# A macaron block on one core: v laid out by head pair and row half, light products with v in 64x64 parts, router in column groups

## The chip, the cores and the metric

The kernel runs on one core of a Trainium2 chip. The metric is the device time of one execution in microseconds. The kernel before took 1715.18 us, the median of 3 runs (1710.5 to 1721.73).

## What is computed

Eight sequences of 1024 rows of 256 numbers, all in 32 bits, go through a feed-forward layer with 8 experts, an attention layer and the same feed-forward layer again. Cut to what matters here:

```
x = x + 0.5 * ffn(layernorm(x))
x = x + attn(layernorm(x))
x = x + 0.5 * ffn(layernorm(x))

ffn:   logits = x @ router_w + router_b            # 256 -> 8
       the two best experts of each row, softmax over the two
       sum of gate * (gelu(x @ W1[e] + b1[e]) @ W2[e] + b2[e])
attn:  light: q, k, v = split(layernorm(x) @ wqkv_l)   # 8 heads of 64
              windows of 64 rows; each attends to itself and to the windows before and after
              softmax(q k^T / 8) @ v, then @ wo_l
       heavy: the 256 best rows for q and the 256 best for k, v, by two scores of each row
              full attention among them, 8 heads of 64, then @ wo_h, added to the rows of q
```

## The kernel before

Everything is written as recorded operations: `record` (line 189, so most profile lines carry L221), `copy` (L304, an eviction from PSUM on VectorE or ScalarE), `scale` (L313, VectorE or GpSimd) and `count`. `Plan` then orders all operations of the program with a list scheduler of its own (`schedule`, line 453; `backward`, 569; `order`, 617). It prices each operation (`Op.cost`, `Engine.work` at line 227 for TensorE, with a fixed charge for a change of the array's shape), looks ahead a number of operations on each engine, chooses VectorE or ScalarE for each eviction and gives PSUM banks of the pool `pmm` in the order in which they come free. What order it starts from is set at the end of `program` (lines 1993 on): each stage (rows, experts, front, heavy, project, light, last sum, dense) has a place and a length in units of one sequence, moved by the table `PLACES` (line 77). Any change of an operation or of a place can so move every instruction on every engine.

PSUM has eight banks of 128 x 512 numbers: `psim` two tiles of two banks (scores), `pmm` three single banks (everything else), `pexp` one (the experts' first product, `ph`). Pools are at lines 685 to 687.

A matmul of 32-bit numbers shows as two records in the profile, a transpose as one. A matmul may use a part of the array: the rows that its contraction needs and the columns that its stationary side needs. "128*64" in a profile line is 128 rows by 64 columns.

The parts that the change and the prediction touch:

- `logits` (line 1176, tiles `pl`): for a group of 4 tiles of 128 rows, 8 matmuls, each with 128 rows of x as the stationary side and the router's 8 columns as the moving side, into one bank; then one addition of the bias on VectorE. It is called from `rows` (line 941, for the 14 routed passes over a sequence) and from `dense` (line 1206, for the first pass of sequence 0 and the last pass of sequence 7, in which all experts are computed).
- `project` (line 1769, tiles `lv`, `lk`, `lq`): v of a tile of 128 rows is two matmuls of 128*128 with 512 moving columns; partition p of `v[:, t, :]` is row p of tile t, all heads side by side.
- `scores_light` (line 1401, tiles `sim_..atl`): for a tile t and a group g of four heads, 24 matmuls at most of 64*64 (row half j is the head of a pair, column half w is the window of queries), with 64, 128 or 192 moving keys. The keys of head j = 0 and j = 1 stand in different orders (`OWN`, `OTHER`, line 1396).
- `soften` (line 1323): one maximum over the four heads on VectorE, four exponentials with sums on ScalarE, a reciprocal, and `scale`.
- `values_light` (line 1438): four transposes of a head's own 128 keys (`keys_first`, tile `pa`), two of the keys beside (tile `pb`), both evicted (`at`, `bt`); then into one bank `pav` four matmuls of 128*64 over the own keys (two at a time, one in each column half) and up to eight of 64*64 over the keys beside, of which row half and column half are always the same, j. Where the window beside lies in the wrong row half of v, its copy `vside` is read, which two DMAs on SyncE's queue make for each tile (`prepare`, line 1827). One eviction makes `loT`, then `lo` multiplies with wo_l.
- `attend_heavy` (line 1360): scores of two head pairs in a `psim` tile, `soften`, eight transposes, the product with v, for 2 tiles of queries and 2 groups in each of 8 sequences: 32 times.

```
psim = nc.pool(ctx, "psim", 2, space=PSUM)
pmm = nc.banked(ctx, "pmm", 3, space=PSUM)
pexp = nc.pool(ctx, "pexp", 1, space=PSUM)
```

Of the kernel before, what the change touches and what calls it, by code (L numbers as in the profile page):

```python
# [44 lines left out]
F32 = mybir.dt.float32  # L45
# [12 lines left out]
P = 128  # L58
# [18 lines left out]
PLACES = {  # L77
    2: (-0.006, 0.000),
    8: (-0.109, 0.000),
    12: (0.000, 0.094),  # L80
    13: (0.143, 0.000),
    16: (0.442, 0.000),
    22: (0.000, -0.182),
    23: (-0.119, -0.119),
    24: (-0.004, 0.000),
    26: (0.000, 0.405),
    31: (0.000, -0.063),
    44: (0.038, 0.000),
    47: (0.000, 0.055),
    48: (0.051, 0.000),  # L90
    54: (0.044, 0.000),
    55: (0.000, -0.120),
    57: (0.040, 0.040),
    62: (0.014, 0.014),
    69: (0.086, 0.000),
    70: (0.403, 0.000),
# [85 lines left out]
class Engine:  # L182
# [44 lines left out]
    def work(method, out, ins, kw):  # L227
# [430 lines left out]
def program(  # L658
# [80 lines left out]
    rw_sb = load(router_w, "rw_sb")  # L739
# [201 lines left out]
    def rows(f, src, group, routed):  # L941
# [11 lines left out]
        rank = small([P, T, E], "erank")  # L953
        for i_b, b in enumerate(group):
# [7 lines left out]
            for hf in range(2):  # L962
# [13 lines left out]
                logits(ls[:, ts(hf, 4), :], yT, 4, f"{n}_{hf}")  # L976
# [184 lines left out]
    def better(ls, rank, tiles, n):  # L1161
# [12 lines left out]
        nc.vector.tensor_reduce(rank, gt, axis=AX.X, op=ALU.add)  # L1174

    def logits(dst, yT, tiles, n):
        pl = bank(f"pl_{n}")
        for i in range(tiles):
            for k in range(KD):
                nc.tensor.matmul(  # L1180
                    pl[:, ts(i, E)],
                    yT[:, k, ts(i, P)],
                    rw_sb[:, k, :],
                    start=(k == 0),
                    stop=(k == KD - 1),
                )
        nc.vector.tensor_tensor(
            dst,
            pl[:, : tiles * E].rearrange("p (t e) -> p t e", e=E),
# [16 lines left out]
    def dense(rows_of, weights, n, yT=None):  # L1206
# [26 lines left out]
        logits(lg, yT, m, n)  # L1233
        rank = sized(two, [P, m, E], F32, "cmp2", f"erank_{n}", NT * slots(MOST) // 2)
# [88 lines left out]
    def soften(sim, keys, n):  # L1323

        nmax = three.tile([P, 4], F32, tag="nmax", name=f"nmax_{n}")
        nc.vector.tensor_reduce(
            nmax.rearrange("p (c j) -> p c j", c=2),
            sim.rearrange("p j c k -> p c j k"),
            axis=AX.X,
            op=ALU.max,  # L1330
            negate=True,
        )
        pool, tag = (one, "ah") if keys > 3 * W else (two, "a")
        a = pool.tile([P, 4, keys], F32, tag=tag, name=f"a_{n}")
        asum = three.tile([P, 4], F32, tag="asum", name=f"asum_{n}")
        for c in range(2):
            for j in range(2):
                i = 2 * c + j
                nc.scalar.activation(
                    a[:, i, :],  # L1340
                    sim[:, j, c, :],
# [713 lines left out]
```

## Time and profile before

| What | Value |
|---|---|
| median of 3 runs | 1715.18 us |
| the profiled execution: its time, its span | 1724.71 us, 1723.0 us |
| granted TensorE clock, mean | 0.988 |
| TensorE busy | 1635.0 us (95%) |
| VectorE, ScalarE, GpSimd busy | 1232.4, 879.8, 836.7 us |
| bytes moved by DMA | 284.60 MB, 165 GB/s mean |
| TensorE busy from 0 to 150 us / 600 to 1100 us | 128.46 us / 483.38 us |

The profile is of one execution, on a clock that starts with its first instruction. "Busy" is the union of the records' times; records of TensorE overlap, so that their durations (about 0.27 us for a 128-column one) are longer than the distance from one start to the next, and it is this distance that counts for throughput. The chain of work that ended last is followed back from the last instruction; a line of it gives start, time until the next piece, and what ran.

### The profile page before, as it was taken

To read this page: it belongs to the slowest core of one execution; us is meant where nothing else is said; L and a number is where in the kernel's file an instruction comes from. 1 tells how busy PE (TensorE), PEld (TensorE's weight loads), DVE (VectorE), ACT (ScalarE), POOL (GpSimd) and SP (SyncE) were. 2 spreads that over 40 slices of the span, in tenths; PEclk is the share of its full clock that TensorE was granted. 3 is DMA by queue.
4 is the path that set the end of the run, shared out by engine and by line. 5 is a ranking of instruction groups with operands and counts; after the bars stand their busy time and mean duration, and the time that the engine had idled before them with its cause. 6 is when DMAs were issued, how large, how long until landed. Compare 5 with 4: busy or idle time off the path is not lost.

```text
span 1723.0 us, 39326 instructions
## 1 busy us (share of the span) xinstructions
PE 1635.0 (95%) x13849; PEld 1221.9 (71%) x13849; DVE 1232.4 (72%) x3881; ACT 879.8 (51%) x2500; POOL 836.7 (49%) x721
## 2 busy tenths in 40 slices
PE   7899999999999999999999999998999999999998
PEld 4566787656777677776777776677677776668786
DVE  6677748798876597658758797547876598568645
ACT  1123737534655565546656545466456554455532
POOL 1050576165553325558466625456373566453424
PEclk9899999999999999999999999999999999999999
DMA  9364786223662335787585623657366555644453
GB/s 190 134 199 152 217 268 196 86 77 118 199 211 74 80 113 158 238 244 228 157 248 173 171 90 108 207 174 230 126 190 198 139 158 181 212 126 129 128 169 113
DMA packets 220037, 284.60 MB, mean 165 GB/s; under 512 B 53448, under 2 KB 160864, under 8 KB 219584
## 3 DMA queue, kind: packets, MB, share of 16 engines
q1 hardware_dynamic: 190896, 208.77, 39.5%
q0 software_dynamic: 28368, 73.31, 15.4%
q8 instruction: 109, 1.79, 0.4%
q14 instruction: 88, 0.72, 0.1%
q10 hardware_dynamic: 576, 0.02, 0.0%
HBM read 196.15 MB, written 80.61 MB: 161 GB/s over the span
## 4 chain that ended last, share of the span: by engine, by line
PE 68%; DVE 15%; DMA 11%; issue 4%; POOL 1%; ACT 1%; SPq 0%; POOLq 0%; DVEq 0%; ACTq 0%
PE po_0f L221 3%; PE ph_0f L221 2%; PE po_7f L221 2%; PE po_2f L221 2%; PE ph_7f L221 2%; PE po_6f L221 2%; PE po_4f L221 2%; PE ph_6f L221 1%; PE ph_4f L221 1%; PE ph_2f L221 1%; DMA got_6at<-ys_6f,at_6f 1%; PE lk_3at L221 1%; DMA xp_6f<-y_6f,token_6f 1%; PE pt_6f L221 1%; PE lk_6at L221 1%
## 5 line engine op out<-in xcount | busy, mean ns | idle before, releaser
L221 POOL DMA_INDIRECT xp_2f<-y_2f,token_2f x78 | 82.2, 1053 | 97.1 <-DVE token_2f L221 40.5
L221 ACT ACT_TABLE_LOAD x75 | 96.2, 1283 | 3.8 <-DVE nmax_5atl L221 1.5
L221 POOL DMA_INDIRECT xp_6f<-y_6f,token_6f x62 | 67.5, 1088 | 53.1 <-PE pt_6f L221 26.0
L221 POOL DMA_INDIRECT xp_4f<-y_4f,token_4f x62 | 66.2, 1068 | 40.6 <-issue 16.3
L221 POOL DMA_INDIRECT xp_0f<-y_0f,token_0f x39 | 40.6, 1040 | 35.2 <-PE pt_0f L221 10.9
L221 PE MATMUL ph_2f<-xTe_2f,wt_2f 128*128 128x128 f32 x312 | 45.5, 279 | 2.6 <-DMA wt_2f<-wpk 2.6
L221 ACT ACTIVATE act_0f<-ph_0f,b_sb 128x512 f32<-128x512 f32 x16 | 11.0, 687 | 70.9 <-PE ph_0f L221 53.2
L221 PEld LDWEIGHTS ph_2f<-xTe_2f,wt_2f 128*128 128x128 f32 x312 | 41.2, 191 | 8.4 <-DMA wt_2f<-wpk 4.9
L221 DVE SCALAR_TENSOR_TENSOR x_last<-po_7f,weight_7f,x_last 128x256 f32<-128x256 f32 x64 | 27.9, 479 | 23.9 <-PE po_7f L221 23.7
L221 PE MATMUL po_2f<-wt_2f,act_2f 128*128 128x256 f32 x156 | 44.5, 381 | 0.3 <-ACT act_2f L221 0.3
L313 POOL TENSOR_TENSOR a_1atl<-a_1atl,asum_1atl 128x768 f32<-128x768 f32 x11 | 17.0, 1544 | 50.9 <-DVE asum_1atl L221 44.0
L221 PE MATMUL ph_0f<-qT,experts 128*128 128x512 f32 x64 | 36.4, 695 | 2.4 <-ACT act_0f L221 2.4
L221 PE MATMUL ph_7f<-yTf_7f,experts 128*128 128x256 f32 x128 | 34.6, 386 | 4.0 <-ACT act_7f L221 4.0
L221 PEld LDWEIGHTS ph_4f<-xTe_4f,wt_4f 128*128 128x128 f32 x248 | 34.1, 191 | 5.6 <-issue 3.7
L221 PE MATMUL ph_4f<-xTe_4f,wt_4f 128*128 128x128 f32 x248 | 37.8, 278 | 0.2 <-DMA wt_4f<-wpk 0.2
L221 PE MATMUL po_0f<-experts,act_0f 128*128 128x256 f32 x128 | 35.7, 384 | 0.9 <-ACT act_0f L221 0.9
L221 ACT ACTIVATE act_7f<-ph_7f,b_sb 128x256 f32<-128x256 f32 x32 | 15.2, 474 | 41.5 <-PE ph_7f L221 25.0
L221 PE MATMUL po_7f<-experts,act_7f 128*128 128x256 f32 x128 | 36.4, 378 | 0.0
L221 POOL DMA_INDIRECT xp_1f<-y_1f,token_1f x23 | 23.9, 1039 | 25.3 <-DVE ends_1f L221 12.7
L221 PE MATMUL ph_6f<-xTe_6f,wt_6f 128*128 128x128 f32 x248 | 35.6, 277 | 0.6 <-DMA wt_6f<-wpk 0.6
L221 PEld LDWEIGHTS ph_6f<-xTe_6f,wt_6f 128*128 128x128 f32 x248 | 32.9, 191 | 4.6 <-issue 2.1
L221 PE MATMUL po_6f<-wt_6f,act_6f 128*128 128x256 f32 x124 | 35.0, 380 | 0.3 <-ACT act_6f L221 0.3
(1493 smaller groups left out, 5800.0 us busy)
## 6 DMA issues: line engine op xcount, KB each, us to landing
wt_2f<-wpk SPq DMA_DIRECT2D x78, 256.5 KB
wt_4f<-wpk SPq DMA_DIRECT2D x62, 256.5 KB
wt_6f<-wpk SPq DMA_DIRECT2D x62, 256.5 KB
wt_0f<-wpk SPq DMA_DIRECT2D x39, 256.5 KB
ys_2f<-yp_2f SPq DMA_DIRECT2D x38, 256.0 KB
ys_4f<-yp_4f SPq DMA_DIRECT2D x30, 256.0 KB
ys_6f<-yp_6f SPq DMA_DIRECT2D x30, 256.0 KB
o<-h_b SPq DMA_DIRECT2D x56, 128.0 KB
```

The lines of the kernel that those rows point to most:

```text
L221: op = Op(self.plan, engines, lambda _: issue(*args, **kw), outs, ins, kind, **how)
L313: return getattr(nc, engine).tensor_tensor(dst, dst, by, op=ALU.mult)
```

## The change

1. v is laid out anew. `project` makes it with matmuls of 128*64: partition half c of `v[:, t, :]` holds, for window w at column 256 w, the 64 rows of the window for the heads of pair c of each group. All keys of a head pair so stand in one row half.
2. `soften` writes the light weights as [64-key block, head pair, pair member, key], so that one transpose gives the keys of pair c = 0 in the upper and those of c = 1 in the lower row half. `values_light` makes six transposes: four into `pa`, two into the columns of the score tile that the scores leave free (`room`, 128 columns of each bank); both are evicted. All products with v are then 64*64: row half c, column half j, four parts one after the other. The two row halves write two banks, `pav[0]` and `pav[1]`, and there are two evictions for `loT`. `pb`, `vside` and its DMAs are gone.
3. The heavy scores no longer lie in `psim` but in two `pmm` banks, one for each j, with a maximum for each.
4. `logits` swaps sides: the router's weights, padded with zeros to 32 columns, are stationary, 128 rows of x move, and tile i goes to column group i. The result is evicted, transposed back and added to the bias. `rank` is written in 16 bits.
5. The planner's price list gets an entry for 32 columns, and `PLACES` goes from 19 entries to 51.

```diff
 PLACES = {
+    0: (-0.035, -0.035),
     2: (-0.006, 0.000),
-    8: (-0.109, 0.000),
...
@@ work @@
+        if cols <= 32:
+            return {"work": n / 2.4, "array": (128, 32)}
         if array == (64, 64):
             return {"work": 58 * n / 64, "array": array}
@@ program @@
-    rw_sb = load(router_w, "rw_sb")
+    rw_sb = cons.tile([P, KD, 4 * E], F32, tag="rw_sb", name="rw_sb")
+    nc.vector.memset(rw_sb, 0.0)
+    nc.scalar.dma_start(out=rw_sb[:, :, :E], in_=router_w)
@@ better @@
-        nc.vector.tensor_reduce(rank, gt, axis=AX.X, op=ALU.add)
+        nc.count(rank, gt)
@@ logits @@
-    def logits(dst, yT, tiles, n):
+    def logits(dst, yT, spare, tiles, n):
         pl = bank(f"pl_{n}")
-        for i in range(tiles):
-            for k in range(KD):
+        for k in range(KD):
+            for i in range(tiles):
                 nc.tensor.matmul(
-                    pl[:, ts(i, E)],
-                    yT[:, k, ts(i, P)],
-                    rw_sb[:, k, :],
+                    pl[4 * E * i : 4 * E * (i + 1), :P],
+                    rw_sb[:, k, :],
+                    yT[:, k, ts(i, P)],
...
+        some = 4 * E * tiles
+        turned = spare[:some, :P]
+        evict(turned, pl[:some, :P])
+        nc.tensor.transpose(pl[:, P : P + some], turned, ident[:some, :some])
         nc.vector.tensor_tensor(
             dst,
-            pl[:, : tiles * E].rearrange("p (t e) -> p t e", e=E),
+            pl[:, P : P + some].rearrange("p (t e) -> p t e", e=4 * E)[:, :, :E],
@@ soften @@
-        a = pool.tile([P, 4, keys], F32, tag=tag, name=f"a_{n}")
+        parts = keys // W if light else 1
+        a = pool.tile([P, parts, 4, keys // parts], F32, tag=tag, name=f"a_{n}")
...
-                    a[:, i, :],
-                    sim[:, j, c, :],
+                    a[:, :, i, :],
+                    sim[j][:, c, :].rearrange("p (b k) -> p b k", b=parts),
@@ attend_heavy @@
-            sim = psim.tile([P, 2, HALF], F32, tag="sim", name=f"sim_{n}_{g}")
-            sim = sim.rearrange("p j (c k) -> p j c k", c=2)
+            sim = [bank(f"sim_{n}_{g}_{j}").rearrange("p (c k) -> p c k", c=2) for j in range(2)]
@@ scores_light @@
         sim = psim.tile([P, 2, HALF], F32, tag="sim", name=f"sim_{n}_{g}")
+        room = sim[:, :, 6 * W :]
...
-            apart = []
             for w in range(2):
                 for j in range(2):
-                    if w in beside and w != j:
-                        score(c, w, j, 0, q0 - W * j, 3 * W)
-                        continue
-                    score(c, w, j, OWN[j], q0, P)
-                    if w in beside:
-                        apart.append((c, w, j, OTHER[j], q0 - W if w == 0 else q0 + P, W))
-            for one_of in apart:
-                score(*one_of)
+                    score(c, w, j, 0, q0, 3 * W if w and w in beside else P)
+            if 0 in beside:
+                for j in range(2):
+                    score(c, 0, j, P, q0 - W, W)
@@ values_light @@
-        at = keys_first(a, OWN, f"{n}_{g}_0")
-        pb = bank(f"pb_{n}_{g}")
...
+        pa = bank(f"pa_{n}_{g}")
+        for i in range(6):
+            to = pa[:, ts(i, P)] if i < 4 else room[:, i - 4]
+            pair = a[:, i // 2, i % 2 * 2 : i % 2 * 2 + 2, :].rearrange("p c k -> p (c k)")
+            nc.tensor.transpose(to, pair, ident)
+        at = three.tile([P, 4, P], F32, tag="at", name=f"at_{n}_{g}")
+        evict(at.rearrange("p i q -> p (i q)"), pa)
+        bt = two.tile([P, 2, P], F32, tag="bt", name=f"bt_{n}_{g}")
+        evict(bt, room)
+        pav = [bank(f"pav_{n}_{g}_{c}")[:, :P] for c in range(2)]
...
+        for w in range(2):
+            for c in range(2):
+                for j in range(2):
+                    value(
+                        c, j, t, w, at[half(c), 2 * w + j, :], slice(0, P), start=(w == 0), stop=False
+                    )
+        for w in beside:
+            for c in range(2):
+                for j in range(2):
+                    value(
+                        c,
+                        j,
+                        t + 2 * w - 1,
+                        1 - w,
+                        bt[half(c), j, half(w)],
+                        half(w),
+                        start=False,
+                        stop=(w == beside[-1]),
+                    )
         for c in range(2):
...
-        evict(loT[:, ts(g, 2), :].rearrange("p c q -> p (c q)"), pav[:, : 2 * P])
+            evict(loT[:, 2 * g + c, :], pav[c])
@@ project @@
-            for k in range(KD):
-                nc.tensor.matmul(
-                    pv,
-                    xT[:, k, ts(t, P)],
-                    wqkv_sb[:, k, 2 * INNER :],
+            for w in range(2):
+                for k in range(KD):
+                    for c in range(2):
+                        of = wqkv_sb[:, k, 2 * INNER :].rearrange("p (g c i) -> p g c i", g=2, c=2)
+                        nc.tensor.matmul(
+                            pv[half(c), ts(w, 2 * P)],
+                            xT[:, k, t * P + w * W : t * P + (w + 1) * W],
+                            of[:, :, c, :],
...
@@ light, prepare @@
-            vside = two.tile([P, KI, DH], F32, tag="vside", name=f"vside_{n}_{t}")
-            for w, src in enumerate((t - 1, t + 1)):
-                if 0 <= src < NT:
-                    nc.sync.dma_start(
-                        out=vside[w * W : (w + 1) * W, :, :],
-                        in_=v[(1 - w) * W : (2 - w) * W, src, :].rearrange(
-                            "p (c j d) -> p c j d", c=KI, j=2
-                        )[:, :, w, :],
-                    )
```

More of the change, by code (lines that the diff above doesn't have):

```diff
@@ L1232, in dense @@
         lg = sized(two, [P, m, E], F32, "cmp2", f"lg_{n}", NT * slots(MOST) // 2)
-        logits(lg, yT, m, n)
-        rank = sized(two, [P, m, E], F32, "cmp2", f"erank_{n}", NT * slots(MOST) // 2)
+        logits(lg, yT, two.tile([P, D], F32, tag="y", name=f"turned_{n}"), m, n)
+        rank = sized(two, [P, m, E], BF16, "cmp2", f"erank_{n}", NT * slots(MOST))
         better(lg, rank, m, n)
```

166 lines of the change are left out of this document (90 added, 76 removed).

## The prediction

> **What bounds the kernel now.** I read the page first: busy times and the shares of the chain.
>
> ```profile
> span 1723.0 us, 39326 instructions
> PE 1635.0 (95%) x13849; PEld 1221.9 (71%) x13849; DVE 1232.4 (72%) x3881; ACT 879.8 (51%) x2500; POOL 836.7 (49%) x721
> ...
> PE 68%; DVE 15%; DMA 11%; issue 4%; POOL 1%; ACT 1%; SPq 0%; POOLq 0%; DVEq 0%; ACTq 0%
> ```
>
> TensorE (PE) is busy 95% of the span and carries 68% of the chain. Next, what TensorE waits for:
>
> ```profile
> PE pt_0f L221 <- DVE y_0f L221: 12.6, 3, 8.7
> PE pt_6f L221 <- DMA xp_6f<-y_6f,token_6f: 5.5, 3, 3.5
> PE ph_7f L221 <- ACT act_7f L221: 4.0, 6, 0.9
> PE ph_1f L221 <- DMA wt_1f<-wpk: 2.8, 1, 2.8
> ```
>
> The longest wait is at the start; then there are only many small ones. So TensorE's throughput is the price of everything. It is read from distances between starts, here from the chain of waits (start, time until the next piece, what):
>
> ```profile
> 328.32 2.10 PE pav_0atl L221 x48
> 1016.79 1.75 PE pl_3f L221 x16
> ```
>
> Sixteen router records take 1.75 us, 0.109 each, though each moves only 8 columns. Two light value steps take 2.10 us. What parts of the array give is in the timeline (start, length, what):
>
> ```profile
> 516.65 1.57 PE L221 MATMUL sim_1atl<-kT,qT 64*64 64x128 f32 x48
> ...
> 792.49 1.09 PE L221 MATMUL pav_2atl<-at_2atl,v 128*64 128x128 f32 x16
> 793.51 0.27 PE L221 MATMUL pav_2atl<-bt_2atl,vside_2at 64*64 64x64 f32 x1
> 793.52 0.27 PE L221 MATMUL pav_2atl<-bt_2atl,v 64*64 64x64 f32 x1
> 793.62 0.22 PE L221 MATMUL pav_2atl<-bt_2atl,vside_2at 64*64 64x64 f32 x1
> 793.63 0.22 PE L221 MATMUL pav_2atl<-bt_2atl,v 64*64 64x64 f32 x1
> 793.68 0.22 PE L221 MATMUL pav_2atl<-bt_2atl,vside_2at 64*64 64x64 f32 x1
> ```
>
> The 16 records over the own keys (128*64) go in pairs, 0.109 from pair to pair: 8 x 0.109 + the last one's length. Those over the keys beside also go in pairs (793.51 and 793.52, 793.62 and 793.63, then 0.059 apart), because only two of the four 64x64 parts are used. The 48 score records, 128 columns in the mean, take 1.57 us: twelve rounds of four at 0.109 plus one length of 0.27 is 1.58. There, four parts do work at once. Between 792.49's last pair (793.31) and 793.51 there are 0.20 instead of 0.109, and the first new pair loses another 0.05: a change of the array's shape costs 0.15 here, up to 0.25 elsewhere; I take 0.19.
>
> I price every matmul in the built order of the kernel before by such rows (128 columns 0.109 a record, 256 columns 0.216, 512 columns 0.429, pairs and fours as above, 425 changes of shape at 0.19). That gives 1582 us of the 1723; 141 are waits, some 20 of them half clock.
>
> **The change, part by part.**
>
> *Values over the keys beside.* 896 matmuls, 1792 records. Now 896 pairs x 0.059 = 52.9; in fours 448 x 0.059 = 26.4. Saved 26.4.
>
> *Values over the own keys.* 1024 records in 512 pairs x 0.109 = 55.8; after, a contraction of 64 needs twice the records, 2048, in 512 fours x 0.109 = 55.8. Nothing. Bounds for both products: four at once as in the score row (26.4 saved together), or only two at once as in the rows of the keys beside (own keys 1024 pairs, 111.6: 55.8 lost together). I take the score row: it has the same parts, two row halves in two banks, back to back.
>
> *Transposes.* 768 before and after. Nothing.
>
> *v.* 128 matmuls x 2 x 0.429 = 109.8 become 512 in pairs of two column halves, 512 pairs x 0.216 = 110.6. Costs 0.8.
>
> *Router.* 512 records x 0.109 = 55.8. After, 512 records in four column groups and 34 transposes x 0.109 = 3.7. No row has column groups of 32. Bounds: four at once, 128 x 0.109 = 14.0, and one at a time, 55.8; with two at a time, 27.9. So -38.1 to +3.7. I take four at once, since column halves overlap fully in the value row and quarters of the array in the score row.
>
> *Changes of shape.* The new built order has 414, among them 72 into or out of the column groups, which are more than paid by the own keys now having the shape of the scores. 11 x 0.19 = 2.1 saved.
>
> Work on TensorE: 26.4 + 38.1 + 2.1 - 0.8 = 65.8 less.
>
> *Evictions and VectorE.* ScalarE gets 109 more copies, VectorE 53 and 32 more maxima (of half the size). The row for a 128x256 copy is 0.37 us on ScalarE, 0.42 on VectorE: below 41 and 36 us, to 55% and 76% of the shorter span. They lie beside TensorE; without that cover, 77. The strided exponentials (row 0.43 each, 512 of them) may cost 0 to 0.1 more, 51 us on an engine that is half idle; 0. The 16-bit rank: 0.
>
> The Trainium skill ("TensorEngine Tiling (Array Packing)", Performance Considerations, PSUM Bottleneck) speaks against the change here: tiling speeds up TensorE but not the emptying of PSUM, which may become the limit. By the rows ScalarE is 51% busy and the copies are covered; if the rule held and the 162 copies stood on the path at 0.37, the sum below would be 60 worse, about 1735.
>
> *DMAs.* 112 issues of vside leave SyncE's queue (0.606 us each, 68 us of the queue; the wt loads and h_a stand behind them). TensorE's waits for DMAs that the view lists sum to about 17 us, a third of it wt. 0 to 5 saved; 2.
>
> *New holds of PSUM.* This is the loss. Heavy scores now keep two of the three pmm banks until their exponentials are done:
>
> ```profile
> 790.34 1.22 DVE L221 TENSOR_REDUCE nmax_3ath<-sim_3ath 128x4 f32<-128x1024 f32 x1
> ...
> 792.95 0.48 ACT L221 ACTIVATE a_3ath<-sim_3ath,nmax_3ath 128x256 f32<-128x256 f32 x1
> ```
>
> From 790.3 to 793.4: 3.1 us, with a signal to TensorE about 3.5. In the new order the TensorE work between the last heavy score in a bank and the next use of that bank is 3.0 us in the median, 1.9 in the lowest tenth; before, the psim tile had 6 us and more. The sum of what lacks to 3.5 is 42 us over 64 banks, 21 a pair. The heavy transposes stand 5.7 us of work behind the scores (median) instead of 13, and need about 6; this is late in the same places. For ordinary evictions (1.1 us needed; 0.8 for the halved pav ones) what lacks grows in pmm from 56 to 66 us, in psim from 0 to 3, where the room must be emptied before the next scores. The router's new transpose waits for its eviction, and the expert products queued behind it on TensorE wait too: 1.15 us of other work stand between in the median, and 6 us lack over 34 calls. Sum: 21 + 10 + 3 + 6 = 40. One wait often serves two tiles, so I take 28. Ends: 0, and 32 holds x 3.3 = 106 with nothing beside them.
>
> *Order and PLACES.* All stages move; what that does is in the counts above, which come from the new order. Start and end look alike: the same first products, dense experts at the end.
>
> Sum: -65.8 - 2 + 28 = -40. Profiled execution 1724.7 -> about 1685; it lay 9.5 above the median, so the median goes from 1715 to **1675**. Its own range, from waits of 10 to 48 (all 40 and a fifth more) and DMAs of 0 to 5: 1654 to 1697.
>
> **The rivals.**
>
> *A. Column groups do not overlap.* For it: no row of 32 columns. Against it: pairs of 64 columns do. Two at a time adds 14, one at a time 42: 1689 to 1717, at the mean 1703. "No change" is the far end, with the evictions added.
>
> *B. Heavy scores starve TensorE (the other side).* Place: 32 holds in the heavy stage, two of three banks gone, one left for everything. Price: up to 3.3 us a hold. It decides from 68 / 32 = 2.1 us a hold, where all that is saved is given back; at 3.3 the time is 1715 - 68 + 106 = 1753. Against it: psim and pexp go on (light scores, first expert products), and 3.0 us of work stand there in the order. For it: VectorE at 76% answers late.
>
> *C. Waits shrink too.* With SyncE's queue lighter and light scores no longer sharing psim with heavy ones, the 141 us of waits don't grow: 1715 - 68 - 5 = 1642.
>
> *D. Value parts run only two at a time.* 1675 + 26 + 56 = 1757. Against it: the score row. I give it 2 in 100, with B.
>
> **How the numbers follow.** Forecast 0.63 at 1675, A 0.13 at 1703, B and D 0.11 above 1715, C 0.13 at 1642. The range takes in forecast, A and C: 1640 to 1712, leaving out B and D, and the ends. Faster by over 1% (about what a measurement of this kernel can tell from no change; below 1698): 0.60 of the forecast, C, and 0.05 of A: 0.78. Within 1%: 0.03 + 0.07 and 0.01 of B: 0.11. Slower: 0.11.
>
> **What would show it.** Right: two value steps are 64 records in about 1.5 us (8 x 0.109 + 8 x 0.059 + 0.15) instead of 48 in 2.10; a router call's 16 records take 0.45 to 0.7 us plus a transpose; TensorE's busy time falls by 50 to 70 us; no vside in the DMA list. Waits of TensorE that name heavy exponentials, a_..ath or nmax_..ath, and evictions of loT sum to some 20 to 40 us. Wrong: pl records 0.109 apart (A); waits of 3 us in each heavy stage (B); value records in pairs (D).

## The result, and the profile after

The changed kernel takes 1775.38 us (median of 4 runs, 1769.31 to 1780.66), the kernel before 1716.98 (4 runs, 1710.5 to 1721.73): a ratio of 1.0342, with a 95% interval from 1.029 to 1.0393. The forecast was 1675, with a range up to 1712. The profiled execution of the changed kernel took 1769.31 us, with a span of 1767.6 and a granted clock of 0.983.

First the page of the changed kernel: span, busy times, and the shares of the chain.

```profile
span 1767.6 us, 42906 instructions
...
PE 1642.7 (93%) x15675; PEld 1239.2 (70%) x15675; DVE 1249.8 (71%) x3964; ACT 925.9 (52%) x2621; POOL 839.9 (48%) x724
...
PE 60%; DVE 15%; DMA 11%; issue 7%; POOL 3%; ACT 2%; SPq 1%; POOLq 0%; DVEq 0%; ACTq 0%
```

TensorE was to lose 50 to 70 us of busy time. It gained 8 (1635.0 to 1642.7), and it also stands idle for longer: by the gaps between its records 112.6 us instead of 74.8. What it waits for (waited for, total, times, longest):

```profile
PE pt_0f L254 <- DVE y_0f L254: 9.9, 2, 8.5
PE pt_2f L254 <- DMA xp_2f<-y_2f,token_2f: 7.8, 3, 3.1
PE pa_7ath L254 <- POOL a_7ath L348: 3.8, 1, 3.8
PE ph_7f L254 <- ACT act_7f L254: 3.7, 7, 0.6
PE pc_6f L254 <- DVE chosen_6f L254: 3.6, 1, 3.6
```

The longest one at the start is as before, one heavy wait in this list is new (pa_7ath), and no wait is large. The prediction named a sign: waits for heavy exponentials (a_..ath) or an eviction of loT would sum to 20 to 40 us. Those over 0.15 us sum to 15.2, against 3.3 before. So both parts of the loss have to be read from distances between starts. Here is the timeline of TensorE where a light step came as the forecast had it (start, length, what):

```profile
511.82 0.67 PE L254 MATMUL pav_1atl<-at_1atl,v 64*64 64x128 f32 x16
512.31 0.41 PE L254 MATMUL pav_1atl<-bt_1atl,v 64*64 64x64 f32 x16
512.54 0.84 PE L254 MATMUL sim_1atl<-kT,qT 64*64 64x128 f32 x24
```

A whole value step, 32 records, takes 0.72 us from 511.82 to 512.54. Two of them would be 1.45, against the 1.5 forecast and 2.10 before. Four parts of 64x64 do work at once here. But 36 us later the same timeline shows this:

```profile
547.77 0.54 PE L254 MATMUL pav_1atl<-at_1atl,v 64*64 64x128 f32 x5
548.05 0.39 PE L254 MATMUL sim_1atl<-kT,qT 64*64 64x128 f32 x3
548.15 0.27 PE L254 MATMUL pav_1atl<-at_1atl,v 64*64 64x128 f32 x1
...
551.12 0.27 PE L254 MATMUL pav_1atl<-at_1atl,v 64*64 64x128 f32 x1
...
551.22 0.60 PE L254 MATMUL pav_1atl<-at_1atl,v 64*64 64x128 f32 x7
551.56 0.48 PE L254 MATMUL pav_1atl<-bt_1atl,v 64*64 64x64 f32 x8
551.98 1.30 PE L254 MATMUL lv_2at<-wqkv_sb,xT_2at 128*64 128x256 f32 x10
```

Two value steps and two score steps are mixed here, and they take 4.21 us (547.77 to 551.98). The last three value lines are sixteen records, half a step: in the built order, the products of one `pav` bank and so of one row half. From 551.12 to 551.98 they take 0.86 us, of which some 0.1 is the change of shape to the projection of v (the last product starts at 551.83, and such records come 0.059 apart). The 0.77 left are as long as the whole step above, though it is half the work: the other row half has nothing to do.

The router, in the same timeline (a value in brackets is the wait ahead of the piece):

```profile
544.23 0.64 PE L254 MATMUL pl_0f<-yTf_0f,rw_sb 128*32 128x128 f32 x16
545.26 0.33 PE L254 MATMUL pl_0f<-ident,yTf_0f 128*128 128x128 f32 x1 [0.39 <-ACT yTf_0f L339]
546.34 0.74 PE L254 MATMUL pa_1atl<-ident,a_1atl 128*128 128x128 f32 x5 [0.75 <-DVE lg_0f L254]
```

The sixteen records are over 0.64 us after the first one's start (before, the next piece began 1.75 us after the first): column groups do overlap. But then TensorE waits 0.39 us for the eviction and 0.75 for VectorE.

The time from one TensorE start to the next, summed from its first record to its last by what the first of the two belongs to, gives the account of the change. A wait counts with the record ahead of it. The last column is the experiment h4, told below, on a chip where the kernel before takes about as long as on the first (h1: 1704.1 in sum).

| TensorE, start to start, us | before | after | h4: products in units of four, old banks |
|---|---|---|---|
| light products with v | 132.7 | 153.2 | 106.1 |
| light scores | 118.0 | 102.5 | 116.5 |
| light transposes | 106.5 | 120.0 | 120.4 |
| router | 58.5 | 39.9 | 36.1 |
| v projection | 114.5 | 117.2 | 118.9 |
| heavy scores, transposes, products | 104.6 | 125.7 | 106.6 |
| experts' second product | 243.2 | 257.7 | 242.1 |
| everything else | 831.1 | 838.9 | 857.5 |
| sum | 1709.1 | 1755.1 | 1704.2 |

Light products and scores together went from 250.7 to 255.7, where 26.4 less were forecast. The router gave 18.6. The heavy stage lost 21.1, light transposes 13.5, the experts' second product 14.5.

### The profile page after: what moved, and what is told of

Read it like the earlier page. It is cut to its first block, busy times and chain, and to the rows that moved or that the text cites. A ratio compares the mean times of both kernels' runs of the same rounds, so it can differ in the third digit from the quotient of the medians.

```text
span 1767.6 us, 42906 instructions
## 1 busy us (share of the span) xinstructions
PE 1642.7 (93%) x15675; PEld 1239.2 (70%) x15675; DVE 1249.8 (71%) x3964; ACT 925.9 (52%) x2621; POOL 839.9 (48%) x724
## 3 DMA queue, kind: packets, MB, share of 16 engines
q0 software_dynamic: 28368, 73.31, 15.2%
## 4 chain that ended last, share of the span: by engine, by line
PE 60%; DVE 15%; DMA 11%; issue 7%; POOL 3%; ACT 2%; SPq 1%; POOLq 0%; DVEq 0%; ACTq 0%
PE po_2f L254 2%; PE po_7f L254 2%; PE ph_2f L254 2%; PE ph_7f L254 1%; PE po_0f L254 1%; PE ph_0f L254 1%; DMA xp_2f<-y_2f,token_2f 1%; DMA wpk<-in_b 1%; PE pav_0atl L254 1%; DMA got_3at<-ys_2f,at_2f 1%; PE po_6f L254 1%; DMA xp_4f<-y_4f,token_4f 1%; PE po_4f L254 1%; PE pav_5atl L254 1%; PE ph_6f L254 1%
## 5 line engine op out<-in xcount | busy, mean ns | idle before, releaser
L254 POOL DMA_INDIRECT xp_2f<-y_2f,token_2f x78 | 88.3, 1132 | 79.0 <-PE pt_2f L254 18.8
L348 POOL TENSOR_TENSOR a_2atl<-a_2atl,asum_2atl 128x768 f32<-128x768 f32 x10 | 15.0, 1500 | 44.6 <-DVE asum_2atl L254 24.9
L254 PE MATMUL po_4f<-wt_4f,act_4f 128*128 128x256 f32 x124 | 35.0, 378 | 0.0
```

Source lines behind the costliest of these rows:

```text
L254: op = Op(self.plan, engines, lambda _: issue(*args, **kw), outs, ins, kind, **how)
L348: return getattr(nc, engine).tensor_tensor(dst, dst, by, op=ALU.mult)
```

## The experiments

Theory 1 says that TensorE lost its fours, because the planner orders every product by itself. Before the change, products over own keys and scores had different shapes, so the planner's charge for a change of shape kept a step together. Now all are 64x64, nothing holds a step together, and the two `pav` banks are two allocations that it opens one after the other. Theory 2 says that the loss is waits: heavy scores and two `pav` banks take the three `pmm` banks, and the new order makes evictions late.

The runs fell on several chips. The kernel before takes 1717 to 1721 us on the first chip and on that of the runs h1 to h4, but 1844 to 1859 on the four others, so each run is given as its ratio to the kernel before on its own chip, with a 95% interval. The expectations of e1 to e4 were written in microseconds of the first chip and are read as differences.

### Four single edits to the changed kernel (e1 to e4)

e1 issues each four of products with v, and each step of scores, as one operation of the planner (a unit). A unit starts when a `pmm` bank is free for each of its new tiles:

```diff
-            nc.tensor.matmul(
-                pav[c][half(j), q], v[half(c), of, at : at + DH], rhs, **flags
-            ).how["work"] = QUARTER * free(rhs) / W
+            four.append((pav[c][half(j), q], v[half(c), of, at : at + DH], rhs, flags))
+            if len(four) == 4:
+                nc.together(four[:], 4 * QUARTER * free(rhs) / W, (64, 64))
+                four.clear()
...
-                        if not free_at or any(asks[i] for i in new):
+                        if len(free_at) < len(new) or any(asks[i] for i in new):
```

> The planner may no longer split them: the four parts of a product with v are one operation, and so are the six scores of a head pair. Nothing is computed differently. Theory 1, broken fours: in the changed kernel the planner mixes the single matmuls of scores and of products with v, since they now have the same shape, and the same part of the array comes twice in a row; its 64x64 stretches took 255.7 us although fours would need about 160. Kept whole, the rounds in the built order price at 190 us instead of 276, so some 60 to 85 us go: 1690 to 1715. Theory 2, new waits (heavy scores in two pmm banks, the new order and its table of places): the parts were not the loss, at most 20 us go: 1755 or more.

e2 puts the old `PLACES` into the changed kernel:

```diff
 PLACES = {
-    0: (-0.035, -0.035),
     2: (-0.006, 0.000),
-    4: (-0.065, -0.088),
...
```

> The changed kernel with the table of places of the kernel before, 19 entries. Theory 1, broken fours: the rounds in the built order price at 284 us, as bad as the 276 of the changed kernel, so 1755 to 1795. Theory 2a, the new table makes the waits: 40 us go, 1740 or less.

e3 brings the old banks back:

```diff
-            sim = [bank(f"sim_{n}_{g}_{j}").rearrange("p (c k) -> p c k", c=2) for j in range(2)]
+            sim = psim.tile([P, 2, HALF], F32, tag="sim", name=f"sim_{n}_{g}")
...
-            to = pa[:, ts(i, P)] if i < 4 else room[:, i - 4]
+            to = pa[:, ts(i, P)] if i < 4 else pb[:, ts(i - 4, P)]
```

> The PSUM moves undone: heavy scores in psim again, the two transposes of the keys beside in a pmm bank pb again. All else as in the changed kernel. Theory 1, broken fours: the rounds price at 288 us, 12 more than in the changed kernel: 1765 to 1800. Theory 2b, heavy scores starve TensorE: their share of the waits goes, 30 to 50 us, 1725 to 1745.

e4 has the old router in the changed kernel:

```diff
-    rw_sb = cons.tile([P, KD, 4 * E], F32, tag="rw_sb", name="rw_sb")
+    rw_sb = load(router_w, "rw_sb")
...
-                    pl[4 * E * i : 4 * E * (i + 1), :P],
-                    rw_sb[:, k, :],
+                    pl[:, ts(i, E)],
                     yT[:, k, ts(i, P)],
+                    rw_sb[:, k, :],
```

> The router as before (x stationary, 8 columns moving, no transpose, 32-bit rank kept at 16 bits); all else as in the changed kernel. The router's records take 39.9 us from start to start in the changed kernel and 58.5 in the one before, changes of shape included; 80 changes of shape fewer (334 instead of 414). If the router part pays as the records say, 19 us are lost, but theory 1 sees rounds of 245 us instead of 276 in this order, 31 less: 1755 to 1775. If the router part alone is what costs (its eviction and its transpose wait in TensorE's queue), 30 us or more go: 1745 or less.

Measured: e1 1.0425 (1.0347 to 1.0503), e2 1.0803 (1.0729 to 1.0877), e3 1.040 (1.033 to 1.047), e4 1.0425 (1.0349 to 1.0501). The changed kernel stands at 1.034 on the first chip, so none of the four edits takes the loss away alone. Read as differences to the changed kernel, e1 lies where theory 2 has it and e3 where theory 1 has it; e4 lies just above theory 1's range, e2 above both. e2 shows only that a list of places belongs to its kernel.

### The same on one chip, and the list and the router alone (f1 to f4)

f1 is the changed kernel itself. f2 is the kernel of e1 on the same chip as f1.

> The changed kernel itself, unaltered, for a trace and a time on the same chip as the runs beside it. Every theory: 1.03 to 1.04 of the kernel before. If this chip is the one of the first four runs (kernel before at 1858 us), the 64x64 stretches will take more than the 255.7 us of the first trace, because TensorE showed pauses there that nothing explains (about 50 us in 100 places).

> The changed kernel with each four of products with v, and each step of six scores of a half, issued as one unit that the planner can't break up; on the same chip as the changed kernel this time. Theory 1 (broken fours): the rounds priced by their longest member are 190.5 us here against 276.1 in the changed kernel, and 45 more changes of shape give back 8.6; so 50 to 75 us below the changed kernel (0.958 to 0.97 of it), about level with the kernel before (0.985 to 1.01). Theory 2 (the loss is waits of the new order and the banks): the order of everything else is as in the changed kernel, so 0.99 to 1.01 of the changed kernel, 1.03 to 1.04 of the kernel before.

f3 is the kernel before with the new router (e4's edit the other way round) and `rank` in 16 bits to make room:

```diff
-        rank = small([P, T, E], "erank")
+        rank = small([P, T, E], "erank", BF16)
```

f4 is the kernel before with the new `PLACES` (e2's edit the other way round).

> The kernel before with the router of the change alone (column groups, four copies of the weights, the turn back, ranks in BF16 to make room). By the rows: router records 38.1 us less, 34 turns 3.7 more; but the planner's order has 498 changes of shape against 425, at 0.19 us 13.9 more, and rounds of the 64x64 stretches at 194.2 against 185.9 us, 8.3 more: sum 12 us less, 0.993 of the kernel before. Theory 1 (the loss sits in the 64x64 stretches, not in the router): 0.985 to 1.005. Rival (the router's turn, its eviction and its waits cost more than its records save): 1.01 to 1.03.

> The kernel before with the list of places of the change: the same instructions in another order. This prices how much of any difference is due to the order's own list being fitted or not fitted to a kernel. Rows: work on TensorE 1584.3 against 1554.8 us (14 more changes of shape, more scores with values in other shapes), so at least 1.017. If lists fitted to one kernel are bad for another as the second run of the first call (changed kernel with the old list, 1.080 against about 1.03 to 1.04) suggests: 1.02 to 1.06. If the list hardly matters: 1.00 to 1.01, and then the second run's loss needs another cause.

Measured: f1 1.0369 (1.0329 to 1.041), f2 1.0395 (1.035 to 1.0439), f3 1.023 (1.0175 to 1.0285), f4 1.0181 (1.0141 to 1.0221). By time alone theory 1 has missed: f2 is no faster than f1. The pages say why. TensorE's row of f1:

```profile
PE 1729.7 (90%) x15675; PEld 1285.6 (67%) x15675; DVE 1249.9 (65%) x3964; ACT 923.4 (48%) x2621; POOL 842.6 (44%) x724
```

and of f2:

```profile
PE 1673.4 (88%) x15675; PEld 1218.0 (64%) x15675; DVE 1255.8 (66%) x3986; ACT 925.1 (48%) x2608; POOL 837.2 (44%) x725
```

Units take 56.3 us off TensorE's busy time, about what theory 1 expected of the whole time (50 to 75); the 64x64 stretches, the time on products and scores in parts of 64x64, fall from 346.3 to 276.3 us. But the idle gaps grow from 169.8 to 225.2, and all is given back. Some of f2's longest waits (total, times, longest):

```profile
PE po_0f L254 <- DVE b_s L254: 11.2, 1, 11.2
...
PE pa_3ath L254 <- POOL a_3ath L348: 5.6, 1, 5.6
PE pa_7ath L254 <- DVE a_7ath L348: 5.2, 1, 5.2
PE lo_4at L254 <- ACT loT_4at_l L339: 5.1, 1, 5.1
```

The first is one wait for the tile b_s, which f1 does not have. The others are of two kinds that do add up: waits over 0.15 us that name an eviction of loT, which empties a value bank, go from 8.1 us in f1 to 30.9, and those that name heavy exponentials from 7.5 to 21.3. That is 36.6 of the 55.4 us. The heavy stage as a whole, start to start, does not grow (138.4 and 139.2). So both theories may hold at once, and the next step is to undo both. f3 is about 33 us above the upper end of what theory 1 gave it, and in the rival's range. But the router's row of the account is short (37.9 us, against 63.3 in f4, which has the old router), so the loss does not lie in the router's own records and the waits behind them. By the planner's own estimate of the end f3 is 61 us behind the kernel before (1733.4 and 1672.9): the list of places does not fit it. g4 below has the old router under an equal estimate. f4 came where its rows had it (1.017), though the planner's estimate puts it 4 us ahead of the kernel before. In f4 an order made for another kernel costs some 2%, and the estimate does not see it.

### Units and old banks together, broken eights, old router (g1 to g4)

g2 has e1's units and e3's banks, with the eight own-key products of a step as one unit; g1 is that with units of four and a list searched for it by the planner's estimate:

```diff
-            if len(four) == 4:
+            if len(four) == (8 if of == t else 4):
```

```diff
-    48: (0.026, 0.000),
...
-    68: (0.115, 0.135),
+    68: (0.070, 0.090),
```

> As the run beside it, with the change's own list of places (planner's estimate 1674.3), and the eight own-key products of a step as one unit: two whole fours, one after the other. Theory 1: 64x64 stretches priced by rounds at 190.5 against 276.1 us in the changed kernel; planner's estimate 7.5 us worse; so 0.99 to 1.015 of the kernel before. Theory 2: 1.03 to 1.04. Against the run beside it: 0 to 14 us slower.

> The changed kernel with fours and score steps as units, the banks as before the change (heavy scores in psim, all six light transposes in pmm banks), and a list of places searched for this kernel with the planner's own estimate of the end (1660.2 us; two entries differ from the change's list; the kernel before stands at 1672.9 in the same estimate, the changed kernel at 1666.8, the unit kernel of the second call at 1721.9). Theory 1 (broken fours, given back in the second call by an order that did not fit the units): the estimate charges fours as whole, which is true here and not in the changed kernel, so 50 to 80 us below the changed kernel and 0.985 to 1.01 of the kernel before. Theory 2 (waits of the changed dataflow, whatever the order): 1.03 to 1.04.

g3 is g2, but inside each eight the same part comes twice in a row:

```diff
             if len(four) == (8 if of == t else 4):
+                if of == t:
+                    four[:] = [four[i] for i in (0, 4, 1, 5, 2, 6, 3, 7)]
```

> The same program as the run before it, instruction for instruction and place for place, but inside each unit of eight own-key products the same part of the array comes twice in a row (first bank's rows, both windows, then the next part). Nothing else moves, so the difference is the price of a broken four alone. Theory 1: five rounds of 0.218 us in place of two in each of 128 steps are 84 us more on TensorE; if only row halves matter, four rounds in place of two, 56 us; some of it covers waits, so the time rises by 30 to 84 us, 1.016 to 1.045 of the run before it. Rival (TensorE sorts the products itself, the order inside a step costs nothing): 0 to 8 us.

g4 has the old router (e4's edit) and g2's steps, but with the eight as two units of four.

> As the second run of this call (its steps in fours, eights split into two units) with the router of the kernel before. By rows TensorE has 25 us more work (1551.3 against 1526.2 with changes of shape, 385 of them against 457) and 34 turns with their waits less; the planner's estimate is equal (1674.2). If the router saves what its records say less its changes of shape: 10 to 25 us slower than the second run. Rival (the router's turn, eviction and changes of shape eat the saving, as the run of the router alone at 1.023 suggests): equal or up to 20 us faster than the second run.

Measured: g1 1.0094 (1.0061 to 1.0128), g2 1.0119 (1.0087 to 1.0151), g3 1.0174 (1.0142 to 1.0207), g4 1.0218 (1.0188 to 1.0248). g1 and g2 are where theory 1 has them, 2.5 to 3 points under f1 and f2. g3 refutes theory 1 as I had put it: the same part twice in a row costs 7 us (1876.35 against 1869.53, hardly clear of the scatter), not 30 to 84; the 64x64 stretches take 275.5 against 270.6. Something sorts eight records of one row half out. g4 is 18.3 us slower than g2 under an equal planner's estimate, within the 10 to 25 expected. Only 11.0 of that stand in the router's row of the account (57.9 against 46.9); light products take 16.1 more, which the split of the eights or the other order may have brought, and other rows take less.

### What breaks the fours (h1 to h4, on a chip like the first)

In the built order of the changed kernel, 3352 of the 6784 records of 64x64 stand in runs of more than eight in one row half. In the kernel before, in f2 and in g3 none do. h2 and h3 test that. h2 issues all sixteen products of a step as one unit, in fours; h3 is the same program, with the first bank's eight ahead of the second's.

```diff
+        four = [p for i, p in enumerate(four) if i % 4 < 2] + [
+            p for i, p in enumerate(four) if i % 4 > 1
+        ]
         work = sum(QUARTER * free(p[2]) / W for p in four)
         nc.together(four, work, (64, 64))
```

> The change with old banks and score steps as units, and all products with v of a step (sixteen, twelve at the edges) as one unit in the order of whole fours. Control of the run beside it. Expected near the run with eights: 1.005 to 1.02 of the kernel before, by either theory.

> The same program as the run before it, instruction for instruction and place for place, except that each unit does the first bank's products first (all in the upper row half) and then the second's (all in the lower), as the planner of the changed kernel does with its two pav banks. Revised theory (each of the four parts has a short queue of about four records, so that one part twice or four times in a row is sorted out, but a run of sixteen records in one row half leaves the other half idle): a sum over the built order with such queues gives 214.6 us for the 64x64 stretches against 168.2, so 46 us more on TensorE, of which some covers waits: 25 to 46 us slower than the run before it, 1.013 to 1.025. If the array's queues are deep (eight records): 4 us. If the order inside a step never costs anything: 0 to 6 us, as in the run with broken eights.

h4 has only the products with v in units of four (e1's diff as shown, with e3's banks), scores one by one; h1 is the kernel before, for its trace.

> The change with old banks and only the products with v as units of four; scores are planned one by one again and may come between two fours. By short queues 177.0 us for the 64x64 stretches against 168.0 with both as units and 215.9 in the changed kernel: revised theory, 0.995 to 1.01 of the run with sixteens. If it were scores between values (and not the runs of one row half) that cost the changed kernel its fours, it would be 20 us or more slower than that run.

> The kernel before itself, for its trace on a chip of the experiments. Both theories: 0.99 to 1.01 of the other runs of it; PE will show pauses that nothing releases, as in the other traces taken outside the first chip, and its 64x64 stretches will take more than the 181.1 us of the first trace.

Measured: h2 1.0039 (1.0019 to 1.0059), h3 1.0138 (1.0098 to 1.0178), h4 1.0023 (0.9993 to 1.0052), h1 1719.12 us beside 1720.59. h2 lies just under its range. h1's expectation missed: this chip is like the first one, without pauses, and its 64x64 stretches take 180.1 us. A step of h2 in the timeline:

```profile
522.15 0.61 PE L412 MATMUL pav_1atl<-at_1atl,v 64*64 64x128 f32 x16
522.59 0.40 PE L412 MATMUL pav_1atl<-bt_1atl,v 64*64 64x64 f32 x16
522.82 0.50 PE L412 MATMUL sim_1atl<-kT,qT 64*64 64x128 f32 x12
```

and one of h3:

```profile
528.42 0.60 PE L412 MATMUL pav_1atl<-at_1atl,v 64*64 64x128 f32 x8
528.86 0.22 PE L412 MATMUL pav_1atl<-bt_1atl,v 64*64 64x64 f32 x2
528.87 0.33 PE L412 MATMUL pav_1atl<-at_1atl,v 64*64 64x128 f32 x2
...
529.36 0.22 PE L412 MATMUL pav_1atl<-bt_1atl,v 64*64 64x64 f32 x2
529.37 0.32 PE L412 MATMUL sim_1atl<-kT,qT 64*64 64x128 f32 x1
529.42 0.28 PE L412 MATMUL pav_1atl<-bt_1atl,v 64*64 64x64 f32 x3
```

In h2 the scores begin 0.67 us after the start of the step, in h3 0.95, and while the step's last products still run. Light products, start to start, go from 115.2 to 157.3 us, scores from 109.1 to 110.9, the 64x64 stretches from 224.3 to 268.2. Of these 44 us, 24 fill gaps in which TensorE stood idle before (122.5 to 98.4), and the time rises by 19.4 us, 1.1%. That is under the 25 to 46 expected, and far from nothing: long runs in one row half cost the fours, and nothing else differs between h2 and h3. The planner of the changed kernel makes such runs. A sum over the built orders in which each part takes up to four waiting records (an estimate, fitted to these traces) gives 168.2 and 214.6 us for h2 and h3, 215.9 for the changed kernel, 141.8 for the kernel before, and 168.0 and 171.8 for g2 and g3; the stretches measured lie 38 to 56 us above it on the two faster chips. It fits; that the parts have such queues is not shown. h4 says that scores between values do no harm: it is as fast as h2.

h4 also shows where the kernel ends up. The page of h1:

```profile
PE 1629.2 (95%) x13849; PEld 1217.1 (71%) x13849; DVE 1233.8 (72%) x3881; ACT 880.9 (51%) x2500; POOL 835.4 (49%) x721
```

and of h4:

```profile
PE 1591.9 (93%) x15675; PEld 1174.9 (68%) x15675; DVE 1240.4 (72%) x3988; ACT 895.1 (52%) x2583; POOL 846.8 (49%) x728
```

TensorE is busy 37.3 us less; its gaps grow by the same (75.3 to 112.7). Waits over 0.15 us that end with VectorE go from 51.5 us in 56 places to 82.1 in 93, the one ahead of TensorE's first record (8.4 and 8.6) included. VectorE does not do more work (1233.8 and 1240.4); it is asked later or in another order. In h4's waits no single one carries this; those that name an eviction of loT sum to 10.1 us against 0.6 in h1, those that name bt to 5.0 against 0.4. Some of them:

```profile
PE pt_0f L254 <- DVE x_0at L254: 5.4, 1, 5.4
...
PE pa_0atl L254 <- DVE loT_0at_l L339: 1.6, 2, 1.4
```

### A fitted list, and units with the new banks (i1, i2)

i1 is h4 with a list of places searched by the planner's estimate. i2 is h4 without e3's edit: h4's units with the changed kernel's banks and list. The longest steps of i1's list:

```diff
-    15: (0.243, 0.210),
+    15: (0.538, 0.210),
...
-    37: (-0.028, 0.014),
+    37: (0.145, 0.187),
```

> The change with old banks and products with v in units of four, as in the run of the values alone (1.0023 of the kernel before), and with a list of places searched for it by the planner's own estimate of the end: 1657.2 us against 1672.2 with the change's list (ten entries differ). If the estimate's difference holds on the chip, 15 us less: 0.99 to 0.997 of the kernel before. If an estimate's 15 us are below what the plan can tell: 0.998 to 1.008.

> The changed kernel with its own banks (heavy scores in two pmm banks, two of the six light transposes in the room of the score tile) and only the products with v as units of four. Against the run of the values alone it differs in the banks only. If the banks give back what the fours save (the second call's unit kernel against the third call's: 1.0395 and 1.012), 1.018 to 1.03 of the kernel before, with heavy scores, transposes and products 15 to 25 us above the 106.6 of that run; the planner's estimates differ by 41 us (1712.9 and 1672.2). If the banks cost nothing here: 1.00 to 1.008, and the changed kernel's 1.034 was the broken fours alone.

Measured on one of the slower chips: i1 1.0081 (1.0051 to 1.0112), i2 1.0422 (1.0367 to 1.0477). Both lie above the ranges written for them. i1's expectation of a gain failed. Whether its list helped at all stays open, since h4 ran on another chip; g1 and g2, on a chip like i1's, are at 1.0094 and 1.0119. i2 is 61.7 us slower than i1. The two differ in the banks and in the list, which the planner's estimate puts at 15 us. The heavy stage, which the banks touch, takes 145.0 us against 108.1, 36.9 of the difference; what the rest is was not separated. In both, the first four of a product must find two of three `pmm` banks free at once; in i2 heavy scores ask for the same three.

Put together, as ratios to the kernel before on the same chip (1.0342 and the last two are from faster chips):

| | products one by one | products in units of four |
|---|---|---|
| new banks | 1.0342, 1.0369 | 1.0395, 1.0422, 1.0425 |
| old banks | 1.040 | 1.0119, 1.0094, 1.0081; 1.0039, 1.0023 on a faster chip |

Neither repair gains anything alone; both together give back three points. The banks are one part of this: f2 and g2 have the same list and router and differ in the banks and in the unit of eight. The planner's estimate, which counts free banks, has f2 47.6 us behind g2 (1721.9 and 1674.3); by their ratios it is some 51. A list fitted to units with the new banks was not tried. The units are the other part, but not by the fours alone. h3, with units but broken fours, is at 1.0138 (on a faster chip), well under e3's 1.040; the clean price of the broken fours is the 1.1% of h3 over h2. What else a unit changes in the order was not separated. By the account, h4 is 50.9 us under the changed kernel: 33.1 in light products and scores, 19.1 in the heavy stage, 15.6 in the experts' second product and 3.8 in the router, less 20.7 elsewhere.

No version was faster than the kernel before; h4 is level with it and about 3% faster than the changed kernel.

## Why the prediction was wrong, point by point

The sum was to fall by 40 us, and the account rose by 46: 86 us off. 31 of these are the fours, 20 the router, 14 the light transposes, 15 the experts' second product; the rest is smaller. The 21 of the heavy stage lie within the 28 forecast for waits.

*Fours.* The first step that failed is "I take the score row: it has the same parts, two row halves in two banks, back to back". The parts do work four at a time when they come so (0.72 us a step), and h4 has the saving as forecast: light products and scores 222.6 us against 250.3 in h1, 27.7 less where 26.4 was forecast. But in the built order they do not come back to back. Products and scores took 5.0 us more, 31 us off. The order was there to be read: I priced each record by its shape from it, and did not ask whether neighbours lie in different row halves. Rival D (two at a time, 2 in 100) has the nearest total (1757), but by luck: it had own keys 55.8 us longer because of the parts, while all light products together took 20.5 us more, because of the order.

*What a saving on TensorE is worth.* The second step that failed is "So TensorE's throughput is the price of everything". h4 has TensorE busy 37.3 us less than h1, and its time is level with the kernel before (1.0023): the gaps grew by as much, and the waits that end with VectorE by 30.6. So even with whole fours and the old banks the time would have been 1721 us by this ratio, not 1675.

*Holds of PSUM.* The heavy stage lost 21.1 us, just what stood for it in the sum of holds. Per hold that is 0.66 us, far under the 2.1 at which rival B decides, so B as priced is refuted. With the old banks (h4) the heavy stage takes 106.6 us, and between f2 and g2 it goes from 139.2 to 119.3, so the loss belongs to the banks. All idle gaps of TensorE grew by 38 us (28 taken, 40 counted). The mechanism was right, and the sum came out partly by luck: the gaps ahead of heavy transposes grew by 12.9, and much of the rest lies where no hold was counted, such as ahead of the experts' transposes (7.4) and their second product (7.3). The Trainium skill ("TensorEngine Tiling (Array Packing)", Restrictions and Gotchas, Gotcha 1: PSUM Pressure) says that row tiling raises the pressure on PSUM, because row tiles write to different banks. The waits that name an eviction of loT, which empties a value bank, point the same way: 0.6 us before, 3.3 after, and 8.1, 30.9 and 41.7 in f1, f2 and g2 on slower chips. No run takes the second value bank away, so its price alone is not shown. What I missed is that such waits leave nothing of a saving elsewhere (f2): freed TensorE time became waiting.

*Router.* Forecast 38.1 less, measured 18.6 in its row of the account, and 11.0 in that row of g2 against g4. Rival A is refuted by the 0.64 us for sixteen records. What lacks: 34 turns took 10.6 us with their waits where 3.7 stood, and the 512 records took 29.3 where 14.0 stood. By an estimate most of that is the 72 changes of shape, at the prediction's 0.19 each 13.7 us, which I had set against own keys that now need none.

*Transposes.* Forecast nothing; they took 13.5 us more, in the changed kernel and in h4 alike, so the room in the score tile is not the cause. The transposes themselves are not slower: what grew is the idle time right behind them, gaps over 0.15 us, from 9.2 to 20.9 us (9.5 in h1, 17.9 in h4). It has many releasers, the largest a DMA with 5.5 us in the changed kernel.

*Changes of shape, v, DMAs, evictions.* v took 2.7 us more (0.8 forecast). TensorE's gaps that end with a DMA went from 19.1 to 17.7 us (2 forecast). ScalarE's busy time grew by 46.1 us (41 forecast), VectorE's by 17.4 (36 forecast); rival C (waits shrink) is refuted.

*Order and PLACES.* "All stages move; what that does is in the counts above": it was not. An order that does not fit costs 1.8% with the same instructions (f4), about as much as the whole change was to bring. The experts' second product, which the change does not touch, took 14.5 us more. The list alone is not the cause: h4 has the same list, and there it takes 242.1 us, as before. Whether the banks or the single products are was not settled.

## What to carry to other kernels

Here parts of the array overlapped only where products for different row halves came close together in the instruction stream (h2 and h3). After a change of layout, read from the built order how long the runs in one half are, and make one unit of what must run together if a scheduler may split it. A saving on the busiest engine counts only while the next resource has room: here time saved on TensorE turned into waits for evictions of the value banks and for heavy exponentials. When two losses cover each other, undoing one can show nothing; undo both before dropping a theory.

## What the runs showed of the hardware

The chips differ. The kernel before took 1717 to 1721 us on the first one and on that of h1 to h4, and 1844 to 1859 on four others, with granted clocks of 0.98 to 0.99 and, in the kernels run on the slower four, 0.94 to 0.97. On the slower ones TensorE shows pauses with no releaser, 38 to 69 us in 61 to 129 gaps over 0.15 us. In f1 40.2 of 49.0 us lie ahead of 64x64 records, in f3 only 7.7 of 38.3. Two of f1's waits:

```profile
PE sim_3atl L254 <- issue: 7.0, 16, 1.0
PE pav_0atl L254 <- issue: 6.3, 5, 4.9
```

On the first chip and that of h1 to h4 they sum to 0.3 us at most. Packets of the queues that load instructions take the same time on both kinds (16 KB: 1.05 us on the first chip, 1.09 in f1), so nothing points there; the cause stays open. The ratios differ too: kernels with units and old banks are at 1.002 to 1.004 on a faster chip and at 1.008 to 1.012 on the slower ones. Why is not shown: f4, with as many 64x64 records as the kernel before, has 54.7 us of such pauses, more than f1.

TensorE evens out eight records in one row half (g3, 5 us on the 64x64 stretches of all 128 steps), but not sixteen (h3, 44 us); lengths between were not run. Records need not start in the order of the program: in h3's step a score starts at 529.37, ahead of products at 529.42 that stand before it in the program and go to another part of the array. Four column groups of 32 overlap: sixteen records in 0.64 us.
